# A decoder layer on one core: the first row tiles issued by two queues, and thirty transposes of the identity ahead of the first real ones

## The chip, the cores and the metric

The kernel runs on one core of a Trainium2 chip. A core has five engines with an instruction queue each: TensorE (PE in the profile; the loading of its weights is shown apart, as PEld), VectorE (DVE), ScalarE (ACT), GpSimd (POOL) and SyncE (SP), which here only issues DMAs. The metric is the device time in microseconds (us) of one execution, as the median of several.

## The reference

One decoder layer in float32 for 16 sequences of 256 tokens with 256 channels (4096 tokens), three parts, each added to its input and normalised:

```python
x = layernorm(x + attn(x))      # fixed keys and values
x = layernorm(x + xattn(x, ctx, ctx, frac))   # 16 heads, softmax, clipped position bias
x = layernorm(x + ffn(x))       # 256 -> 1024 -> 256, top-1 of 8 low-rank experts

def attn(r):                    # 4 heads of 64 channels
    q = (normalise(r) * ln_g + ln_b) split in heads
    k = w_fc.reshape(-1, 64)                  # 1024 keys, no projection of tokens
    v = w_proj.T.reshape(-1, 64)
    return r + square(relu(q @ k.T)) @ v
```

The change touches only the beginning of `attn` for the first 512 tokens.

## The kernel before

The tokens are handled in eight blocks of 512, each as four row tiles of 128 tokens x 256 channels. The program is in three stages: the first attention over the eight blocks (until about 257 us), the cross attention over 64 groups of heads, in whose gaps the feed-forward part of finished blocks is placed, and the feed-forward part of what is left. All is written out by hand in one order (`tc.manual_schedule()`, L895); each engine executes its own instructions in the order in which the Python program emits them, and waits by semaphores for what it needs. Other things than order are not planned.

The start, in the order of emission (L896 to L901):

- `rows_in[0].load()` (L257 to L263): the first block's four row tiles, each 128 KB, as four DMAs on SP's queue.
- `load_first()` (L81 to L84): the keys `kT` as two DMAs of 256 KB on SP's queue (the same keys for both halves of the partitions), and the values `vv`, 256 KB, on ACT's queue. Ahead of these, at L75 to L78, ACT has already issued the two small columns `ln_g` and `ln_b` (1 KB each) and the load of its function table.
- `rows_in[1].load()`: the second block, one DMA of 512 KB on SP's queue.
- `rows_in[0].begin()` (L275): mean and variance of each row tile on DVE (`row_stats`, L187 to L190), the inverse root by a logarithm and an exponential on ACT and three small DVE steps (`inv_std`, L192 to L210), a fourth for the shift (L244), then the rows scaled: tiles 0 and 1 on ACT (L249), tiles 2 and 3 on DVE (L287).
- `turn_in(0)` and `turn_in(1)` (L292): four transposes each on PE, of the scaled rows against the identity `ident` (L295), then gain and shift on the way out of PSUM, by ACT (L299) for the first half of the channels, by DVE (L304) for the second.

The identity is made by POOL among its first instructions (L61 to L62, `make_identity`).

Then the loop over blocks (L916), eight steps `m` for each. A step emits two `scores` (L309: four matmuls of 64 x 64 x 512 in the quarters of the array into one of two PSUM buffers, relu on ACT at L322, the square on DVE at L324), then the two `values` (L327) of the step before, then other work of that step from the list `steps`: `load_cross` (L110: weights and constants of the cross attention, all on SP's queue) in step 0 of block 0, `load_ffn` in step 2, statistics of the next block in steps 3 and 4. `values` adds up in two PSUM tiles, `tile_v()` and `tile_v("W")`.

A float32 matmul appears in the profile as two rows; a transpose as one. So one `scores` is eight rows of L314, in two groups of four that start within 20 ns of each other.

Of the kernel before, what the change touches and what calls it, by code (L numbers as in the profile page):

```python
# [9 lines left out]
FP = mybir.dt.float32  # L10
# [3 lines left out]

P = 128
EPS = 1e-5
CLAMP = 0.2
BIG = 3.0e38

# [2 lines left out]
def tile_decoder_layer(ctx: ExitStack, tc: tile.TileContext, a: dict, out: bass.AP):  # L22


    nc = tc.nc
# [4 lines left out]
    CC = C // P  # L30
# [9 lines left out]
    const = ctx.enter_context(tc.tile_pool(name="const", bufs=1))  # L40
# [16 lines left out]
    def tile_v(tag="V"):  # L57
        return psV.tile([P, 512], FP, tag=tag, name="ps_v")


    ident = const.tile([P, P], FP, name="ident")  # L61
    make_identity(nc, ident)  # L62
    epst = const.tile([P, 1], FP, name="epst")
    nc.gpsimd.memset(epst, EPS)
    rev = const.tile([P, 4, E], FP, name="rev")
    for e in range(E):
        nc.gpsimd.memset(rev[:, :, e : e + 1], float(E - e))
    def columns(name, src, eng):
        t = const.tile([P, src.shape[1]], FP, name=name)
        eng.dma_start(out=t, in_=src)  # L70
        return t


    kT = const.tile([P, 4, C], FP, name="kT")
    ln_g = columns("ln_g", a["ln_g"], nc.scalar)  # L75
    ln_b = columns("ln_b", a["ln_b"], nc.scalar)

    nc.scalar.preload_act_table_set("natural_log_exp_and_others")  # L78
    vv = const.tile([P, CC, C], FP, name="vv")

    def load_first():  # L81
        for h in range(2):
            nc.sync.dma_start(out=kT[64 * h : 64 * h + 64], in_=a["kT"])
        nc.scalar.dma_start(out=vv, in_=a["vv"].rearrange("(c p) f -> p c f", p=P))  # L84


    W = E + ER
    wq, wk, wv, wo = (const.tile([P, CC, C], FP, name=n) for n in ("wq", "wk", "wv", "wo"))
# [20 lines left out]

    def load_cross():  # L110
        load = nc.sync.dma_start
        for t, n in ((wk, "wkT"), (wv, "wvT"), (wq, "wqT")):
            load(out=t, in_=a[n].rearrange("(c p) f -> p c f", p=P))
        for t, n in ((bq, "bq"), (bk, "bk"), (fcol, "frac_cols")):
            load(out=t, in_=a[n])
        for t, n in (
            (bo, "bo"), (apos, "alpha_pos"), (aneg, "alpha_neg"), (gamma, "gamma"),
            (delta, "delta"),
        ):
            load(out=t, in_=a[n].to_broadcast(list(t.shape)))  # L120

        wo_view = a["woT"].rearrange("(o g i d) f -> i g d o f", o=CC, g=4, i=2)
        bv_view = a["bv"].rearrange("x (o g i d) -> i g d (x o)", o=CC, g=4, i=2)
        for i in range(2):
            for g in range(4):
                rows = slice(64 * i + 16 * g, 64 * i + 16 * g + 16)
                load(out=wo[rows], in_=wo_view[i, g])
                load(out=bvc[rows], in_=bv_view[i, g])
# [74 lines left out]
    def newton(mv, near, n):  # L203

        t = small.tile([P, n], FP, tag="sd", name="sd")
        nc.vector.scalar_tensor_tensor(t, mv[:, :, 1], EPS, near, ALU.add, ALU.mult)
        nc.vector.scalar_tensor_tensor(t, t, -0.5, near, ALU.mult, ALU.mult)
# [13 lines left out]
    x_view = a["x"].rearrange("(b j p) c -> b p j c", j=4, p=P)  # L221

    def tile_x():
        return px.tile([P, 4, C], FP, tag="x", bufs=3, name="x")
# [11 lines left out]
    if True:  # L236
# [16 lines left out]
        class Block:  # L253
# [3 lines left out]
            def load(self):  # L257
                self.x = tile_x()
                if self.tb:
                    nc.sync.dma_start(out=self.x, in_=x_view[self.tb])  # L260
                else:
                    for j in range(4):
                        nc.sync.dma_start(out=self.x[:, j, :], in_=x_view[0, :, j, :])  # L263

            def measure(self, jj):
                for j in range(2 * jj, 2 * jj + 2):
# [114 lines left out]
        rows_in = [Block(tb) for tb in range(NB)]  # L381
# [5 lines left out]
    if True:  # L387

        vaug = []
        for i in range(2):  # L390
            t = const.tile([P, 2, NH, 2 * HD], FP, name=f"vaug{i}")
# [4 lines left out]
        class Batch:  # L396
# [107 lines left out]
            def clip(self, name):  # L504

                t = self.cut(name, *((0.0, -CLAMP) if name == "dneg" else (CLAMP, 0.0)))
                if 2 <= self.b < MADE:
# [386 lines left out]

    with tc.manual_schedule():  # L895
        rows_in[0].load()  # L896
        load_first()
        rows_in[1].load()
        rows_in[0].begin()
        rows_in[0].turn_in(0)  # L900
        rows_in[0].turn_in(1)  # L901
# [14 lines left out]
        for tb in range(NB):  # L916
# [63 lines left out]
            for m in range(8):  # L980
                c, n2 = divmod(m, 4)
# [279 lines left out]
```

## Time and profile before

| | us |
|---|---|
| median of 3 runs (lowest, highest) | 914.74 (914.54, 915.02) |
| the profiled execution | 914.93 |
| its span, first to last instruction | 913.1 |
| TensorE busy | 892.4 |
| first matmul | 8.60 |
| first scores (L314) | 10.77 |
| first values (L334) | 16.52 |
| last matmul ends | 907.8 |

All times within a run count from the start of the span. Rows of the time line give start, busy time, engine (SPq and ACTq are the queues from which SP and ACT issue DMAs), line, operation and tiles, how many instructions are merged, and in brackets how long the engine rested before and what ended that rest. Rows of a line by form give, for instructions of one form in a window, how many, then the least, median and longest duration in ns, and first and last start. A matmul's row begins when PE takes it up; rows overlap, so the distance between starts shows the pace.

### The profile page before, as it was taken

To read this page: it belongs to the slowest core of one execution; us is meant where nothing else is said; L and a number is where in the kernel's file an instruction comes from. 1 tells how busy PE (TensorE), PEld (TensorE's weight loads), DVE (VectorE), ACT (ScalarE), POOL (GpSimd) and SP (SyncE) were. 2 spreads that over 40 slices of the span, in tenths; PEclk is the share of its full clock that TensorE was granted. 3 is DMA by queue.
4 is the path that set the end of the run, shared out by engine and by line. 5 is a ranking of instruction groups with operands and counts; after the bars stand their busy time and mean duration, and the time that the engine had idled before them with its cause. 6 is when DMAs were issued, how large, how long until landed. Compare 5 with 4: busy or idle time off the path is not lost.

```text
span 913.1 us, 19025 instructions
## 1 busy us (share of the span) xinstructions
PE 892.4 (98%) x6910; PEld 541.6 (59%) x6910; DVE 707.7 (78%) x1968; ACT 584.2 (64%) x977; POOL 379.5 (42%) x369
## 2 busy tenths in 40 slices
PE   6999999999999999999999999999999999999997
PEld 2333333333356776577658757865875686586555
DVE  5788899889878998778777877777787787678443
ACT  4757877787687879466666856665685567556111
POOL 1002312231469996434635543463454336244010
PEclk9999999999999999999999999999999999999999
DMA  5411011100001222010111202011120201111001
GB/s 137 146 36 35 30 36 41 65 1 2 3 11 50 70 71 56 13 42 21 35 43 39 52 13 66 18 37 41 40 52 14 65 17 40 41 27 45 23 1 47
DMA packets 44190, 37.01 MB, mean 41 GB/s; under 512 B 14912, under 2 KB 40000, under 8 KB 44096
## 3 DMA queue, kind: packets, MB, share of 16 engines
q1 hardware_dynamic: 43536, 35.52, 14.0%
q8 instruction: 55, 0.90, 0.4%
q14 instruction: 39, 0.32, 0.1%
q10 hardware_dynamic: 560, 0.26, 0.1%
HBM read 21.07 MB, written 6.03 MB: 30 GB/s over the span
## 4 chain that ended last, share of the span: by engine, by line
PE 56%; ACT 4%; DVE 1%; issue 1%; ACTq 0%; DVEq 0%
PE ps_b L860 12%; PE ps_l L830 12%; PE ps_b L649 9%; PE ps_l L609 6%; PE ps_v L665 5%; PE ps_b L561 3%; PE ps_b L457 2%; PE ps_b L479 2%; PE ps_l L842 2%; ACT ps_l L600 2%; ACT pT L656 1%; PE ps_b L437 1%; PE ps_b L749 1%; ACT qT L447 1%; DVE neg L624 1%
## 5 line engine op out<-in xcount | busy, mean ns | idle before, releaser
L588 POOL TENSOR_SCALAR neg<-dneg,aneg,delta 128x512 f32<-128x512 f32 x205 | 175.7, 869 | 211.2 <-ACT pT L656 185.8
L624 DVE CUSTOM_DVE_ANT_0 neg<-ps_l,neg 128x256 f32<-128x256 f32 x512 | 181.6, 420 | 43.0 <-PE ps_l L609 39.8
L600 ACT ACTIVATE ps_l<-dpos,apos_d 128x512 f32<-128x512 f32 x256 | 173.1, 686 | 34.5 <-DVE mx L624 30.5
L656 ACT ACTIVATE pT<-ps_b 128x512 f32<-128x512 f32 x256 | 143.3, 590 | 59.1 <-PE ps_b L649 57.4
L324 DVE TENSOR_TENSOR pr<-r 128x1024 f32<-128x1024 f32 x128 | 155.5, 1255 | 32.4 <-ACT r L322 32.1
L322 ACT ACTIVATE r<-ps_a 128x1024 f32<-128x1024 f32 x128 | 126.5, 1022 | 59.1 <-PE ps_a L314 33.9
L649 PE MATMUL ps_b<-ident,neg 128*128 128x128 f32 x1024 | 140.3, 278 | 4.0 <-ACT pT L656 2.4
L649 PEld LDWEIGHTS ps_b<-ident,neg 128*128 128x128 f32 x1024 | 112.9, 140 | 41.9 <-issue 15.3
L639 POOL TENSOR_TENSOR neg<-neg,mx 128x1024 f32<-128x1024 f32 x65 | 124.3, 1914 | 30.0 <-DVE mx L624 24.0
L314 PE MATMUL ps_a<-xnT,kT 64*64 64x512 f32 x1024 | 124.2, 601 | 0.0
L334 PE MATMUL ps_v<-pr,vv 64*64 64x512 f32 x1024 | 123.5, 593 | 0.3
L860 PE MATMUL ps_b<-wof,hT 128*128 128x256 f32 x512 | 115.8, 380 | 0.0
L830 PE MATMUL ps_l<-xt,wi 128*128 128x512 f32 x256 | 115.0, 596 | 0.8 <-ACT hT L849 0.8
L860 PEld LDWEIGHTS ps_b<-wof,hT 128*128 128x128 f32 x512 | 96.4, 190 | 16.0 <-issue 2.3
L639 DVE TENSOR_TENSOR neg<-neg,mx 128x1024 f32<-128x1024 f32 x63 | 90.9, 1443 | 0.3
L349 POOL TENSOR_TENSOR xt<-xt,half 128x512 f32<-128x512 f32 x15 | 23.7, 1583 | 141.0 <-ACT half L348 141.0
L334 PEld LDWEIGHTS ps_v<-pr,vv 64*64 64x64 f32 x1024 | 38.1, 132 | 70.7 <-issue 43.7
L314 PEld LDWEIGHTS ps_a<-xnT,kT 64*64 64x64 f32 x1024 | 38.1, 135 | 67.9 <-issue 56.2
L830 PEld LDWEIGHTS ps_l<-xt,wi 128*128 128x128 f32 x256 | 46.8, 190 | 52.0 <-issue 45.8
L609 PE MATMUL ps_l<-kM,qT 32*128 32x256 f32 x1024 | 74.8, 401 | 0.4 <-ACT ps_l L600 0.4
L665 PE MATMUL ps_v<-pT,vaug 128*32 128x256 f32 x1024 | 69.8, 385 | 0.8 <-ACT pT L656 0.8
L853 DVE TENSOR_SCALAR hT<-ps_l,wib 128x512 f32<-128x512 f32 x44 | 30.5, 745 | 42.8 <-PE ps_l L842 42.8
(107 smaller groups left out, 966.9 us busy)
## 6 DMA issues: line engine op xcount, KB each, us to landing
cT<-in_ctxT SPq DMA_DIRECT2D x16, 256.0 KB
kM<-keys SPq DMA_DIRECT2D x128, 32.0 KB
v<-raw SPq DMA_DIRECT2D x128, 32.0 KB
invs<-rows SPq DMA_DIRECT2D x128, 32.0 KB
x<-in_x SPq DMA_DIRECT2D x7, 512.0 KB
out<-x SPq DMA_DIRECT2D x7, 512.0 KB
frow<-in_frac SPq DMA_DIRECT2D x16, 128.0 KB
wi<-in_wiT SPq DMA_DIRECT2D x1, 1024.0 KB
```

What stands on the lines that cost most here:

```text
L314: nc.tensor.matmul(sc[64 * k : 64 * k + 64, h, :], lhsT=kT[64 * h : 64 * h + 64, q, hf * P + 64 * k : hf * P + 64 * k + 64], rhs=self.xnT[ ...
L324: nc.vector.tensor_tensor(pr, r, r, ALU.mult)
L334: nc.tensor.matmul(self.acc[k][64 * h : 64 * h + 64, :], lhsT=vv[64 * k : 64 * k + 64, hf, 64 * q : 64 * q + 64], rhs=pr[64 * k : 64 * k + ...
L588: nc.gpsimd.tensor_scalar(self.neg[:, g], self.batch.dneg, aneg[:, h : h + 1], delta, ALU.mult, ALU.mult,)
L600: nc.scalar.activation(banks[g], self.batch.dpos.rearrange("p j k -> p (j k)"), AF.Copy, scale=apos_d[:, h : h + 1],)
L609: nc.tensor.matmul(banks[g][:, j * S : (j + 1) * S], lhsT=self.batch.qT[rows, self.o, j * P : (j + 1) * P], rhs=self.batch.kM[rows, self.i ...
L624: nc.vector.tensor_tensor_reduce(out=self.t[:, g, j, :], in0=banks[g][:, j * S : (j + 1) * S], in1=self.neg[:, g, j, :], scale=1.0, scalar ...
L639: eng.tensor_tensor(rows, rows, top.to_broadcast([P, 4, S]), ALU.subtract)
L649: nc.tensor.transpose(ps[:, k * S + j * P : k * S + (j + 1) * P], self.t[:, g, j, k * P : (k + 1) * P], ident,)
L656: nc.scalar.activation(self.pT[:, g, :], self.ps[g], AF.Exp)
L830: nc.tensor.matmul(banks[g], lhsT=wi[:, c, f * P : (f + 1) * P], rhs=self.xT[:, c, :], start=(c == 0), stop=False,)
L860: nc.tensor.matmul(ps[:, 0:C], lhsT=self.hT[f][:, j * P : (j + 1) * P], rhs=wof[:, f, :], start=(f == 0), stop=(f == FC - 1),)
```

## The change

- Row tiles 1 and 3 of the first block are issued by ACT, tiles 0 and 2 by SP.
- The second block's load follows directly on SP's queue.
- `ln_g`, `ln_b` and the table load are issued behind ACT's two row tiles; the keys `kT` move from SP's queue to ACT's, behind these.
- The values `vv` move from ACT's queue to SP's, as the first of `load_cross`.
- Thirty transposes of the identity against itself are put on PE's queue ahead of the first real ones. They write in turn the four quarters of one PSUM tile, of the tag "W", that nobody reads.

```diff
+WARM = 30
-    def columns(name, src, eng):
-        t = const.tile([P, src.shape[1]], FP, name=name)
-        eng.dma_start(out=t, in_=src)
-        return t
...
-    ln_g = columns("ln_g", a["ln_g"], nc.scalar)
-    ln_b = columns("ln_b", a["ln_b"], nc.scalar)
-
-    nc.scalar.preload_act_table_set("natural_log_exp_and_others")
+    ln_g, ln_b = (const.tile([P, CC], FP, name=n) for n in ("ln_g", "ln_b"))
     vv = const.tile([P, CC, C], FP, name="vv")
 
     def load_first():
+        for t, n in ((ln_g, "ln_g"), (ln_b, "ln_b")):
+            nc.scalar.dma_start(out=t, in_=a[n])
+
+        nc.scalar.preload_act_table_set("natural_log_exp_and_others")
         for h in range(2):
-            nc.sync.dma_start(out=kT[64 * h : 64 * h + 64], in_=a["kT"])
-        nc.scalar.dma_start(out=vv, in_=a["vv"].rearrange("(c p) f -> p c f", p=P))
+            nc.scalar.dma_start(out=kT[64 * h : 64 * h + 64], in_=a["kT"])
...
     def load_cross():
         load = nc.sync.dma_start
-        for t, n in ((wk, "wkT"), (wv, "wvT"), (wq, "wqT")):
+        for t, n in ((vv, "vv"), (wk, "wkT"), (wv, "wvT"), (wq, "wqT")):
             load(out=t, in_=a[n].rearrange("(c p) f -> p c f", p=P))
...
                     for j in range(4):
-                        nc.sync.dma_start(out=self.x[:, j, :], in_=x_view[0, :, j, :])
+                        eng = nc.scalar if j % 2 else nc.sync
+                        eng.dma_start(out=self.x[:, j, :], in_=x_view[0, :, j, :])
...
     with tc.manual_schedule():
         rows_in[0].load()
+        rows_in[1].load()
         load_first()
-        rows_in[1].load()
+
+        idle = tile_v("W")
+        for j in range(WARM):
+            nc.tensor.transpose(idle[:, j % 4 * P : (j % 4 + 1) * P], ident, ident)
         rows_in[0].begin()
         rows_in[0].turn_in(0)
         rows_in[0].turn_in(1)
```

## The prediction

> **What bounds the kernel now.** I read the page first: how much room TensorE (PE) leaves, and where. Then the busy time by stretch.
>
> ```profile
> PE 892.4 (98%) x6910; PEld 541.6 (59%) x6910; DVE 707.7 (78%) x1968; ACT 584.2 (64%) x977; POOL 379.5 (42%) x369
> ```
>
> In the stretches the first number is the length, the second PE's busy time, the one before the last two the clock column.
>
> ```profile
> 0.00:8.60 8.60, 0.00 (x0) 0.03 (x1) 3.70 (x14) 2.53 (x5) 3.84 (x20) 1.00 0.70 192
> 8.60:15.10 6.50, 6.48 (x29) 2.76 (x32) 2.05 (x3) 2.72 (x4) 0.00 (x0) 1.00 0.65 185
> 15.10:100.00 84.90, 84.87 (x766) 31.82 (x758) 71.57 (x115) 58.70 (x79) 11.11 (x9) 1.00 0.21 62
> ```
>
> PE works 892.4 of 913.1 us. Of the 20.7 us it rests, 8.60 are the start and 5.3 the end (its last matmul is over at 907.8); from 15.1 to 100 it rests 0.03 us, from 100 to 300 2.3, to 600 3.0, to 907.8 1.5. So PE sets the end, the other engines follow it, and what is won or lost before about 18 us is carried to the end: in between there is hardly any rest in which a shift could drown.
>
> Then the time line of the start, and the matmuls of line 314 by form in three short windows.
>
> ```profile
> 2.97 0.43 DVE L189 BATCH_NORM_STATS2 st<-x 128x6 f32<-128x256 f32 x1 [2.97 <-DMA x<-in_x]
> ...
> 5.76 0.43 DVE L189 BATCH_NORM_STATS2 st<-x 128x6 f32<-128x256 f32 x1 [0.22 <-DMA x<-in_x]
> ...
> 8.60 2.15 PE L295 MATMUL ps_b<-ident,xn 128*128 128x128 f32 x8 [8.60 <-ACT xn L249]
> ...
> 8.81 0.33 SPq L120 DMA_DIRECT2D bo<-in_bo  x1
> ...
> 9.94 0.78 ACT L299 ACTIVATE xnT<-ps_b,ln_b,ln_g 128x512 f32<-128x512 f32 x1 [0.99 <-PE ps_b L295]
> ...
> 10.77 5.93 PE L314 MATMUL ps_a<-xnT,kT 64*64 64x512 f32 x32
> ...
> 18.23 1.90 PE L314 MATMUL ps_a<-xnT,kT 64*64 64x512 f32 x16
> ...
> 37.23 1.09 PE L295 MATMUL ps_b<-ident,xn 128*128 128x128 f32 x8
> ```
>
> ```profile
> L314 PE MATMUL ps_a<-xnT,kT x4: 1021/1026/1031, 14.2 to 14.3; 64*64 64x512 f32 x4
> ...
> L314 PE MATMUL ps_a<-xnT,kT x8: 597/814/1031, 14.2 to 15.1; 64*64 64x512 f32 x8
> ...
> L314 PE MATMUL ps_a<-xnT,kT x4: 589/589/589, 16.1 to 16.1; 64*64 64x512 f32 x4
> ```
>
> The same eight transposes take 2.15 us at 8.60 and 1.09 at 37.23. The same group of four matmuls takes about 1.03 us at 14.2 and 0.59 at 16.1, and groups follow each other every 0.85 us before 15.1 and every 0.43 after. PE runs at half speed up to 15.1 and at full speed from there. The clock column of the stretches reads 1.00 all along, so it does not show this; the durations do. Lifted once, the clock stays up to the last matmul.
>
> So the start has two costs: PE has nothing to do before 8.60, and then 6.5 us of it run at half speed. The chain behind 8.60: the fourth row tile lands (5.76), statistics until 6.40, logarithm and exponential on ACT and four small DVE steps until 7.82, the scaled rows, transposes.
>
> **The rows.** Now SP issues the four tiles one after the other (0.73 to 2.53 on its queue, 0.45 us each) and the values, issued by ACT at 1.68, share the wires with tiles three and four. After the change each queue issues two tiles, by 1.65, with nothing large in front. The first tile can't land earlier than now (2.97). DVE takes 0.56 us per tile (2.97, then 3.53), so with all tiles there in time the fourth begins at 2.97 + 3 x 0.56 = 4.65, 1.11 us before 5.76. Everything behind keeps its distances: the scaled rows would reach PE at 8.60 - 1.11 = 7.49. The other bound is no gain at all (8.60), if the second block's 512 KB, now directly behind on SP's queue, delays the third tile. I take 7.49, but see below: it decides nothing in the likeliest case.
>
> **The thirty transposes.** They stand in front of the real ones on PE's queue and wait only for the identity, which POOL finishes at 2.15 + 0.29 = 2.44; I let them start at 2.50. At half speed one follows another every 0.213 us (9.48, 9.70, 9.91 in the trace; so 2.15 us for eight with a first gap), at full speed every 0.109. All cold: 30 x 0.213 = 6.40, and PE is free at 8.90. That is later than the rows (7.49), so the work put in to fill a pause overruns it; the real transposes, their conversion on ACT and the scores queue behind it. Their output bank is used next by the value sums of the same engine, and in the built order no instruction of another engine waits for it.
>
> The question is whether they lift the clock. Row: PE began at 8.60 and was lifted at 15.1, 6.5 us later, or 4.3 us after its first true matmul at 10.77. The Trainium skill, "TensorE: Matmul & The Clock Gate", Part 1, says that about 3.4 us of sustained work, counted in windows that run freely, lift the clock; so 3.4 to 6.8 us after the start. Part 4 of the same page speaks against this change: transposes don't count as busy in the same way, and full clock doesn't engage for them. The trace fits both: by Part 1 the 6.5 us count from the transposes, with a window that ended at 11.7 only about three quarters filled (gaps at 8.8 and 10.6); by Part 4 the 4.3 us count from the matmuls. Part 4 gives for one transpose 275 ns, most of it read latency[...]; here they run gapless, each starting while the last is in flight, as the matmuls do. I take Part 1, without certainty.
>
> With windows of 3.4 us back from 15.1 (an estimate from that page and this trace) one ends at 4.9, too soon after 2.50 to be full, the next at 8.3. If they lie so again, 27 transposes are cold (2.50 to 8.27), three warm, and PE is free at 8.6. The ends, for windows that lie otherwise: lifted at 5.9, free at 5.9 + 14 x 0.109 = 7.4; or lifted only at 9.3, free at 8.9.
>
> **From the rows to the steady state.** Real transposes from 8.60, now warm: four in about 0.65 us, so ACT starts at 9.25 rather than 9.94, takes 0.78, and the scores start at 10.08 rather than 10.77: 0.69 us won. Then the fill of the pipeline, counted from the scores' start s at full speed: the second group of the first scores starts at 0.43 and ends 0.59 later, so relu (1.02, the next 0.97) runs 1.04 to 2.06 and to 3.03; the fourth scores wait for the second relu and run 3.07 to 3.93; squares on DVE (1.2 each) end at 3.33 and 4.53; the first values start at 3.93, the second wait for their square, 4.57 to 5.43; the fifth scores start at s + 5.43. In the trace that is 18.23 - 10.77 = 7.46. Won: 2.03 us, less than half of the cold stretch, because relu and squares do not speed up and become what the fill waits for. Fifth scores at 10.08 + 5.43 = 15.51, against 18.23: **2.7 us** in all. From there PE is full as before.
>
> **Keys and values.** The keys move from SP behind ACT's two row tiles, the two small columns and the table load; in the built order each of their two issues also waits for a row tile to land, about 3.0 and 3.6. Behind them on ACT's queue stands the logarithm, due at 5.40; 0.6 us per issue ends by about 4.3, so it isn't held. The table load (1.28) then lies at about 2.5 to 3.8, hidden too. The keys landed by 8.8 (SP's issue at 8.81 waited for them) and were wanted at 10.77. Now they share the wires with SP's 512 KB of rows, the values and three weights. Together these are 2.6 MB, as before, and the last of them landed at 12.4. An even share brings the keys' 0.52 MB at half of about 0.28 MB per us (5 to 10 us: 278 GB/s) from 4.3 on to 8.0, with about 0.5 for landing 8.5; both ends: 7.5, and 12.4 if everything else were served first. I take 8.5, before 10.08. The values follow the rows on SP and are wanted at about 14 rather than 16.5; second in that queue, they land before 10. The weights behind are first used tens of us later.
>
> **Sum.** 2.7 us less: span 910.4, the profiled execution 914.93 - 2.7 = 912.2. That execution lies 0.2 over the median of the runs, 914.74, which gives **912.0**. With the windows otherwise: lifted at 5.9, rows at 7.49 decide, scores at 8.97, 1.80 + 2.03 = 3.8 won, 910.9; lifted at 9.3, scores at about 10.4, 2.3 won, 912.4.
>
> **Rivals.** (1) The transposes do not lift the clock (0.35). PE is free at 8.90, real transposes cold without the gap at 8.8: four starts to 9.55, ended 9.97, ACT to 10.80, scores at 10.85 against 10.77, lift near 15.1 as now. All that the rows won is eaten by PE's own queue: 914.8. For it: Part 4, and that the trace has no lift at 11.7. (2) Keys late (0.08): ACT's queue is served behind SP's, PE has the converted rows at 10.03 and stands. While it stands the clock may fall; then the fill costs 7.46 again, and the kernel is slower once the keys land after 10.77, or after 18.23 - 5.43 = 12.8 if the clock holds. Keys at 12.4, clock fallen: 12.4 + 7.46 = 19.9, 1.6 later, 916.4. Against it: half a share suffices with 1.5 us to spare. (3) Rows no earlier (within the likeliest case): with PE free at 8.6, rows at 8.60 and 9.0, 0.4 less, 912.4.
>
> **How the numbers follow.** Lifted 0.57, 910.9 to 912.4 with 912.0 the likeliest; not lifted 0.35, 914.8, by where the windows fall some 0.6 either way; keys late 0.08, up to 916.4. A measurement here can tell about 0.2%, or 1.8 us, from no change. Every lifted case is beyond that; 0.02 off for a cost unseen gives faster 0.55. The unlifted case but for 0.01, and half of the keys, are within it: 0.38. Slower by more has the rest, 0.07. Cases of both signs hold the chance, so the range takes in both: 910.8 to 915.4; the likeliest case alone has 910.9 to 912.5.
>
> **What would show it.** Right: the identity's transposes 0.21 us apart and then 0.11, the eight real ones in about 1.1 us, groups of line 314's work 0.43 apart from the first, the fifth scores near 15.5. Wrong: spacing of 0.21 through all thirty and scores cold until about 15 (rival 1); PE idle between conversion and scores, released by the keys' transfer (rival 2). A fourth tile's statistics later than 4.7 would put the rows' step wrong. A fall of 2.7 at 15.5 that is not there at the end would put the claim wrong that PE carries a shift through.

## The result, and the profile after

The changed kernel takes 916.72 us (median of 12 runs, 915.41 to 917.40), the kernel before in the same comparison 914.58 (913.71 to 915.02): a ratio of 1.0023 [1.0015, 1.0032]. It is slower by 2.1 us, just over what a measurement can tell, where 912.0 was forecast. The profiled execution took 916.48 us with a span of 914.7, 1.55 us longer than before's 914.93.

The first row of the page, as it was read before:

```profile
PE 897.3 (98%) x6940; PEld 552.5 (60%) x6940; DVE 706.9 (77%) x1968; ACT 584.3 (64%) x977; POOL 379.5 (41%) x369
```

PE has its thirty instructions and 4.9 us of work more, and its idle time is 3.3 us less, so the span grew by the rest. The time line of the start says where. Its columns are the start, the busy time, and in the bracket what ended the idle time before it; rows of one kind that follow each other are joined. Because the change shifts the code, rows' statistics are now line 185, the transposes 292, the conversion 296 and the scores 311; line 109 is SP's load of the values and weights, line 80 ACT's load of the keys, line 256 the second block's, line 899 the thirty transposes.

```profile
1.64 0.43 SPq L256 DMA_DIRECT2D x<-in_x  x1
...
2.11 0.51 SPq L109 DMA_DIRECT2D vv<-in_vv  x1
...
2.49 5.72 PE L899 MATMUL ps_v<-ident 128*128 128x128 f32 x30 [2.49 <-POOL ident masks.py:199]
...
3.32 0.43 DVE L185 BATCH_NORM_STATS2 st<-x 128x6 f32<-128x256 f32 x1 [3.32 <-DMA x<-in_x]
...
3.49 1.17 ACTq L80 DMA_DIRECT2D kT<-in_kT  x2
...
4.94 0.40 DVE L185 BATCH_NORM_STATS2 st<-x 128x6 f32<-128x256 f32 x1
...
8.05 1.09 PE L292 MATMUL ps_b<-ident,xn 128*128 128x128 f32 x8
...
8.74 0.78 ACT L296 ACTIVATE xnT<-ps_b,ln_b,ln_g 128x512 f32<-128x512 f32 x1 [0.64 <-PE ps_b L292]
...
11.91 6.40 PE L311 MATMUL ps_a<-xnT,kT 64*64 64x512 f32 x32 [2.77 <-DMA kT<-in_kT]
...
12.96 0.21 PEld L311 LDWEIGHTS ps_a<-xnT,kT 64*64 64x64 f32 x8 [0.89 <-DMA kT<-in_kT]
...
19.71 2.03 PE L311 MATMUL ps_a<-xnT,kT 64*64 64x512 f32 x16
```

Up to the conversion on ACT nothing is lost against the forecast. The fourth tile's statistics start at 4.94 (5.76 before, 4.65 forecast), but the conversion starts at 8.74, where 9.25 was forecast. The thirty transposes take 5.72 us, where 6.4 would mean half speed all along, and the eight real ones take 1.09 us instead of 2.15: the clock is up, and ACT's half of the converted rows is there at 9.52. Then PE stands for 2.77 us, released by the keys' transfer. The keys come in two halves, one for each half of the partitions: the first lets two matmuls go at 11.91, the second the rest at 12.96. Before, they had landed by 8.8. The fifth scores, at 18.23 before and forecast at 15.51, start at 19.71.

The bytes that each queue moved, from the changed kernel's DMA view between 4.3 us (where the forecast let the keys begin) and 12.2 (where their last packet ends); the columns are packets, MB, and the share of the 16 DMA engines' time. The first row is the queue that SP issues to, the second ACT's:

```profile
q1 hardware_dynamic: 1875, 1.49, 72.1%
q10 hardware_dynamic: 446, 0.53, 30.3%
```

Together 2.02 MB in 7.9 us, 0.256 MB per us: close to the 0.28 of the forecast. ACT's queue got 0.53 of the 2.02, a quarter and not half. But this quarter is the mean of two stretches that have little in common. The first pair of rows is from 4.3 to 7.0 us, the second from 7.0 to 12.2:

```profile
q1 hardware_dynamic: 801, 0.79, 92.8%
q10 hardware_dynamic: 287, 0.00, 6.0%
...
q1 hardware_dynamic: 1074, 0.70, 61.3%
q10 hardware_dynamic: 159, 0.52, 42.9%
```

In the first, ACT's queue delivers only the two columns, 256 pieces of 8 bytes, and SP's queue moves almost three packets for each packet of ACT's. In the second the keys move, in pieces of 4 KB, and they get 0.52 of 1.22 MB: 0.43, not far from half. So the keys lost more by beginning late than by a small share.

And the stretches (length, then busy time and count of PE, PEld, DVE, ACT and POOL, the clock column, the DMA share, GB/s):

```profile
9.10:11.90 2.80, 0.04 (x1) 0.02 (x1) 0.83 (x2) 0.41 (x1) 0.00 (x0) 1.00 1.04 218
11.90:13.90 2.00, 1.98 (x13) 0.55 (x16) 0.00 (x0) 0.00 (x0) 0.00 (x0) 1.00 0.35 81
13.90:17.30 3.40, 3.40 (x22) 1.06 (x19) 1.67 (x2) 2.05 (x2) 0.00 (x0) 0.50 0.20 33
```

PE is idle from 9.1 to 11.9, and 2.0 us after it has begun again its clock falls to 0.50, for one stretch of 3.4 us. So the pause costs twice: the wait, and a piece of the clock that the thirty transposes had just bought.

### The profile page after: what moved, and what is told of

Read it like the earlier page. It is cut to its first block, busy times and chain, and to the rows that moved or that the text cites. A ratio compares the mean times of both kernels' runs of the same rounds, so it can differ in the third digit from the quotient of the medians.

```text
span 914.7 us, 19082 instructions
## 1 busy us (share of the span) xinstructions
PE 897.3 (98%) x6940; PEld 552.5 (60%) x6940; DVE 706.9 (77%) x1968; ACT 584.3 (64%) x977; POOL 379.5 (41%) x369
## 4 chain that ended last, share of the span: by engine, by line
PE 56%; ACT 3%; DVE 1%; issue 1%; ACTq 0%; DVEq 0%
PE ps_b L857 12%; PE ps_l L827 12%; PE ps_b L646 9%; PE ps_l L606 6%; PE ps_v L662 5%; PE ps_b L558 3%; PE ps_b L476 2%; PE ps_b L454 2%; PE ps_l L839 2%; ACT ps_l L597 1%; PE ps_b L434 1%; ACT pT L653 1%; PE ps_b L746 1%; ACT qT L444 1%; PE ps_b L421 0%
## 5 line engine op out<-in xcount | busy, mean ns | idle before, releaser
L311 PEld LDWEIGHTS ps_a<-xnT,kT 64*64 64x64 f32 x1024 | 41.4, 134 | 67.7 <-issue 52.4
L331 PEld LDWEIGHTS ps_v<-pr,vv 64*64 64x64 f32 x1024 | 41.0, 132 | 67.8 <-issue 39.1
```

Of the source, the lines that this page charges most:

```text
L311: nc.tensor.matmul(sc[64 * k : 64 * k + 64, h, :], lhsT=kT[64 * h : 64 * h + 64, q, hf * P + 64 * k : hf * P + 64 * k + 64], rhs=self.xnT[ ...
L331: nc.tensor.matmul(self.acc[k][64 * h : 64 * h + 64, :], lhsT=vv[64 * k : 64 * k + 64, hf, 64 * q : 64 * q + 64], rhs=pr[64 * k : 64 * k + ...
```

## The experiments

Two theories of why the keys are late. **A, the front of ACT's queue**: the two columns `ln_g` and `ln_b`, 128 pieces of 8 bytes each, stand directly in front of the keys. Their packets take from 4.29 to 6.94 here (2.10 to 3.15 before), and the keys' own from 7.01 to 12.17. **B, what SP now sends early**: freed of two row tiles and the keys, SP issues the second block at 1.64 and the values at 2.11, with the weights behind: about 1.5 MB beside or ahead of the keys. A third question is what each other part of the change is worth. "Before" in each line is the kernel before in the same comparison.

**1. The keys ahead of the columns, same queue.**

```diff
     def load_first():
+        for h in range(2):
+            nc.scalar.dma_start(out=kT[64 * h : 64 * h + 64], in_=a["kT"])
         for t, n in ((ln_g, "ln_g"), (ln_b, "ln_b")):
             nc.scalar.dma_start(out=t, in_=a[n])
...
-        for h in range(2):
-            nc.scalar.dma_start(out=kT[64 * h : 64 * h + 64], in_=a["kT"])
```

> The changed kernel with one thing moved: on ACT's queue the two key transfers are issued before the two small columns (1 KB each) instead of behind them. Theory A (the keys are late because they stand behind the small columns, whose 8-byte packets crawl between SP's large ones): the keys land by about 8.5 us, scores start by 9.5 instead of 11.9, the clock holds, and the fifth scores start near 15 instead of 19.7: about 4.5 us less than the changed kernel, 912. Theory B (the keys are late because SP's second block, values and weights share the wires, in whatever order ACT issues): the keys still land after 11, and the time stays at 916 to 917. Risk for both: the columns now come last, and the conversion that needs them waits.

Measured: 916.01, ratio 1.0013 [1.0006, 1.0020]; the profiled execution, 913.98, is among the fastest of its 21 (913.75 to 917.81), so the view shows the kind of the wait and not its usual length. The keys are now in time (packets 4.98 to 8.83). Its time line shows the conversion:

```profile
10.76 0.78 ACT L296 ACTIVATE xnT<-ps_b,ln_b,ln_g 128x512 f32<-128x512 f32 x1 [2.02 <-DMA ln_b<-in_ln_b]
```

What stood second in ACT's queue is late instead: the columns hold the conversion for 2.02 us, and the scores start at 11.59. A swap inside the queue moves the wait to another load. Neither theory is separated by it, but a queue in which whatever comes last is late speaks for B.

**2. The thirty transposes alone, added to the kernel before.**

```diff
+        idle = tile_v("W")
+        for j in range(WARM):
+            nc.tensor.transpose(idle[:, j % 4 * P : (j % 4 + 1) * P], ident, ident)
         rows_in[0].begin()
```

> The kernel before with the thirty transposes alone; all DMAs as before. Both theories of the keys expect them at about 8.8, in time. If the transposes lift the clock and the loss of the changed kernel is the keys' alone: real transposes from about 8.6, scores near 10.1, fifth scores near 15.5, 2.7 us less than before, 911.9. Rival theory C (the transposes themselves cost, because the clock they lift falls again before the work comes): clock at half speed again in the fill, 914.5 to 916.

Measured: 912.93, ratio 0.9981 [0.9972, 0.9989], so 1.8 us faster than before's 914.72. In its profile (913.92):

```profile
2.49 5.13 PE L903 MATMUL ps_v<-ident 128*128 128x128 f32 x30 [2.49 <-POOL ident masks.py:199]
```

5.13 us for thirty is again less than 6.4: the clock lifts, here about 5.9 us into the program. In this execution the rows landed late (fourth tile 6.79, before 5.76), which is why its span shows less than the median.

**3. The changed kernel without the thirty transposes.**

```diff
-        idle = tile_v("W")
-        for j in range(WARM):
-            nc.tensor.transpose(idle[:, j % 4 * P : (j % 4 + 1) * P], ident, ident)
```

> The changed kernel without the thirty transposes: its DMA order alone. Theories A and B: scores wait for the keys until about 11.9 as in the changed kernel, now cold, the fill takes 7.5 us as before, fifth scores near 19.4: 1.1 us slower than before, 915.7, and up to 1 us faster than the changed kernel or equal to it, since there most of the fill was cold too. If the transposes' lift still helped in the changed kernel, this is slower than it, 917.5.

Measured: 917.28, ratio 1.0025 [1.0017, 1.0033]; profiled 917.57.

```profile
12.48 6.90 PE L311 MATMUL ps_a<-xnT,kT 64*64 64x512 f32 x32 [2.62 <-DMA kT<-in_kT]
```

The wait for the keys is there without the transposes: 2.62 us. So the new order of the loads makes the loss. Compared with the changed kernel, the transposes bring 0.6 us where they brought 1.8 alone; 0.6 is too little to be told from nothing by the intervals of the two runs.

**4. The changed kernel with the keys back on SP's queue, ahead of the second block.**

```diff
-            nc.scalar.dma_start(out=kT[64 * h : 64 * h + 64], in_=a["kT"])
+            nc.sync.dma_start(out=kT[64 * h : 64 * h + 64], in_=a["kT"])
...
         rows_in[0].load()
-        rows_in[1].load()
         load_first()
+        rows_in[1].load()
```

> The changed kernel with the keys back on SP's queue, in front of the second block; the split of the rows, the values' place and the transposes stay. Theories A and B both expect the keys early (about 6 to 7.5), since nothing large or small stands in front of them but two row tiles: real transposes at about 8.0, scores near 9.5, fifth scores near 15: 3.3 us less than before, 911.3. If moving the keys is not the cause of the loss, the time stays near 916.7.

Measured: 912.34, ratio 0.9971 [0.9960, 0.9982]; profiled 912.21. Its time line:

```profile
1.64 1.21 SPq L80 DMA_DIRECT2D kT<-in_kT  x2
...
2.49 4.85 PE L899 MATMUL ps_v<-ident 128*128 128x128 f32 x30 [2.49 <-POOL ident masks.py:199]
...
9.69 1.95 PE L311 MATMUL ps_a<-xnT,kT 64*64 64x512 f32 x16 [0.43 <-ACT xnT L296]
...
15.47 1.90 PE L311 MATMUL ps_a<-xnT,kT 64*64 64x512 f32 x16
```

PE is released by the conversion, not by a DMA; the fifth scores start at 15.47, 2.76 us before those of the kernel before. In this profile all of the forecast gain is there once the keys come in time; by the medians it is 914.72 - 912.34 = 2.4 of the 2.7, and 1.0 less than was expected of this run.

**5. The columns on SP's queue, behind the second block.** If A is the cause, this cures it.

```diff
-            nc.scalar.dma_start(out=t, in_=a[n])
+            nc.sync.dma_start(out=t, in_=a[n])
```

> The changed kernel with the two small columns issued on SP behind the second block, so that on ACT's queue the keys follow the row tiles directly; keys, values and transposes otherwise as changed. Theory A (the small columns in front hold up the keys): the keys begin at about 4.5 to 5 and land by about 9.3, as with the keys first; the columns now crawl behind 512 KB on SP but come before 9; scores at 9.5 to 10, fifth scores near 15.2, 912 to 912.5. Theory B (SP's large transfers starve whatever ACT issues): keys land after 11, 916 or more.

Measured: 913.17, ratio 0.9985 [0.9978, 0.9991]; profiled 913.15. The keys are in time, but the columns again are not: the conversion waits 1.58 us for `ln_b` and starts at 9.72.

```profile
9.72 0.78 ACT L296 ACTIVATE xnT<-ps_b,ln_b,ln_g 128x512 f32<-128x512 f32 x1 [1.58 <-DMA ln_b<-in_ln_b]
```

It looks like a vote for A, and it isn't a clean one: the columns in SP's queue also put off the values (issued at 3.53 instead of 2.11) and the weights behind them (4.14 instead of 3.31, and so on), which is what B calls for.

**6. The gap filled: 28 more transposes between the real ones and the first scores**, to see what the fall of the clock costs.

```diff
         rows_in[0].turn_in(1)
+        for j in range(28):
+            nc.tensor.transpose(idle[:, j % 4 * P : (j % 4 + 1) * P], ident, ident)
```

> The changed kernel with 28 more transposes of the identity, about 3.05 us at full speed, placed between the real transposes and the first scores, where TensorE stood waiting for the keys. The DMAs are not touched, the keys still land near 11.9. If the clock falls because TensorE stood (theory: the fall costs most of what the transposes had won), it now holds through the fill: scores at 12.0, fifth scores near 12.0 + 5.4 = 17.4 instead of 19.7, 914.4. If the fall costs little or comes from elsewhere: 916.7, as the changed kernel.

Measured: 915.55, ratio 1.0010 [1.0003, 1.0016]; profiled 916.44.

```profile
13.90:17.30 3.40, 3.12 (x26) 0.91 (x30) 1.21 (x2) 1.94 (x2) 0.00 (x0) 1.00 0.23 38
```

```profile
13.90 1.94 PE L311 MATMUL ps_a<-xnT,kT 64*64 64x512 f32 x14 [0.64 <-DMA kT<-in_kT]
...
19.66 1.90 PE L311 MATMUL ps_a<-xnT,kT 64*64 64x512 f32 x16
```

The clock column stays at 1.00 where the changed kernel had 0.50. The keys' second half came at 13.90, the fifth scores 5.76 later at 19.66; in the changed kernel the same step took 19.71 - 12.96 = 6.75. So the fall cost the changed kernel 1.0 us in its profile. By the medians the filling gained 1.2, not the 2.3 that was expected of it: the wait itself stays.

**7. As 4, without the thirty transposes.**

```diff
-            nc.tensor.transpose(idle[:, j % 4 * P : (j % 4 + 1) * P], ident, ident)
```

> The kernel with the keys on SP in front of the second block (912.3 with transposes), now without the thirty transposes: the split rows alone, on a cold clock. Rows reach TensorE about 0.8 earlier than before, scores near 9.9, the fill cold, 7.5: fifth scores near 17.4, 0.8 less than before, 913.9. If the rows' split is worth nothing without the transposes: 914.7.

Measured: 914.10, ratio 0.9993 [0.9985, 1.0001]; profiled 913.39. Rows on two queues are worth about 0.5 us alone, which can't be told from nothing by this interval. Between 7 and 4 the transposes give 914.10 - 912.34 = 1.8, the same as in run 2.

**8. The columns at the very front of ACT's queue**, ahead of its row tiles.

```diff
     with tc.manual_schedule():
+        for t, n in ((ln_g, "ln_g"), (ln_b, "ln_b")):
+            nc.scalar.dma_start(out=t, in_=a[n])
         rows_in[0].load()
```

> The changed kernel with the two small columns at the head of ACT's queue, before its row tiles, as they stood in the kernel before. Theory A: early, with little else on the wires, they cost about 1 us; the keys begin at about 5 and land by 9.5; row tiles 1 and 3 come 0.9 later, so scores near 10.5, fifth scores near 16, 913. Theory B: keys after 11, 916 or more.

Measured: 914.79, ratio 1.0003 [0.9995, 1.0011]; the profiled execution, 913.96, is again among the fastest, here of 13 (913.94 to 915.72). The keys are in time in it, and now ACT's row tiles are late: the fourth tile's statistics start at 6.96 instead of 4.94, the scores at 11.61.

```profile
6.96 0.43 DVE L183 BATCH_NORM_STATS2 st<-x 128x6 f32<-128x256 f32 x1
```

It is the third load in turn that is late for its place.

**9. SP's stream held back**: everything on SP from the second block on is issued only after the first rows' statistics (a write of one column on DVE makes it wait); ACT's queue stays as changed, columns in front.

```diff
+                if self.tb == 1:
+                    nc.vector.memset(self.x[:, 0, 0:1], 0.0)
                 if self.tb:
                     nc.sync.dma_start(out=self.x, in_=x_view[self.tb])
...
                 for jj in range(2):
                     self.measure(jj)
+                rows_in[1].load()
...
         rows_in[0].load()
-        rows_in[1].load()
```

> The changed kernel, but SP's second block is issued only after the statistics of the first rows: a one-column memset on VectorE, put right behind them, makes its issue wait until about 5.5, and the values and weights behind it on SP's queue with it. ACT's queue is as changed, columns in front of the keys. If the columns crawl only because SP's large packets run beside them: columns done within 1 to 1.5 us as in the kernel before, keys begin near 4.5 and land by 8.5 to 9, scores near 9.5, fifth scores near 15, 912.3. If the order on ACT's queue alone delays the keys (8-byte packets slow by themselves, or the late issue behind the table load): keys still land after 10.5, 915 or more. Values and second block now land later, by about 9 to 10, still before their use at 13.5 and 26.

Measured: 912.23, ratio 0.9974 [0.9965, 0.9983]; profiled 912.51. Its time line, where the scores are now line 314:

```profile
2.67 1.82 ACTq L80 DMA_DIRECT2D kT<-in_kT  x2
...
6.13 0.39 SPq L258 DMA_DIRECT2D x<-in_x  x1
...
10.09 1.95 PE L314 MATMUL ps_a<-xnT,kT 64*64 64x512 f32 x16 [0.43 <-ACT xnT L299]
...
15.87 1.90 PE L314 MATMUL ps_a<-xnT,kT 64*64 64x512 f32 x16
```

And its DMA view between 2.6 and 6.9 us, in which the columns and all of the keys move (the columns from 3.33 to 4.82, 1.5 us against 2.65 in the changed kernel, the keys from 3.98 to 6.89, 2.9 us against 5.2):

```profile
q10 hardware_dynamic: 699, 0.75, 61.3%
q1 hardware_dynamic: 194, 0.17, 11.4%
```

With the same queue in the same order the keys come five microseconds earlier, because nearly nothing of SP's is on the wires. This is the run that decides for B: the columns still stand in front, and the time is that of run 4 (912.34) within the noise.

**10. The columns replaced by constants**, 1 and 0, set on DVE, with no DMA at all; this leaves the gain and shift of the first norm out.

```diff
-        for t, n in ((ln_g, "ln_g"), (ln_b, "ln_b")):
-            nc.scalar.dma_start(out=t, in_=a[n])
+        nc.vector.memset(ln_g, 1.0)
+        nc.vector.memset(ln_b, 0.0)
```

> The changed kernel without the two small columns' loads: gain and shift are set to 1 and 0 by VectorE, so that part of the computation is left out; keys, values, rows and transposes as changed. If the columns are what stands in front of the keys: keys begin at about 4 and land by 9 to 9.5, nothing waits for columns, scores at 9.2 to 9.7, fifth scores near 15, 912. If SP's traffic alone is enough to hold the keys: keys land after 11, 916 or more.

Measured: 915.72, ratio 1.0014 [1.0007, 1.0021]; profiled 915.48. A row of its time line, then of its list of waits over the first 20 us (total, times, longest):

```profile
12.49 1.94 PE L311 MATMUL ps_a<-xnT,kT 64*64 64x512 f32 x14 [1.48 <-DMA kT<-in_kT]
```

```profile
PE ps_a L311 <- DMA kT<-in_kT: 2.2, 2, 1.5
```

With nothing in front, the keys' packets begin at 5.16 instead of 7.01, and yet end at 11.94 instead of 12.17; PE still waits 2.2 us for them. By the medians this run is 1.0 us faster than the changed kernel (916.72 to 915.72), of 4.4 that lie between that and run 4. So A alone is not the cause. But 1.0 us is not the price of the columns either, because the edit changes SP's stream too. First a row of the changed kernel's list of SP's waits, then two of this run's DMA view between 5.2 and 11.9 us:

```profile
SPq L109 <- DMA ln_g<-in_ln_g: 2.3, 1, 2.3
```

```profile
q1 hardware_dynamic: 1473, 1.14, 70.1%
q10 hardware_dynamic: 157, 0.52, 27.6%
```

In the changed kernel SP waits 2.3 us for the first column before it issues the third weight, at 6.83. Without columns it issues it at 4.26, and 1.14 MB instead of 0.70 move beside the keys. Run 5 also takes the columns from ACT's queue, but puts the values off: there the keys move from 3.79 to 9.52, and the time is 2.6 us shorter.

**11. Only values and weights held**, until the first rows' statistics; the second block goes at once.

```diff
                 for jj in range(2):
                     self.measure(jj)
+                nc.vector.memset(vv[:, 0, 0:1], 0.0)
```

> The changed kernel with the values, and the three weights behind them on SP's queue, held until the statistics of the first rows (a one-column memset on VectorE, near 5.5); the second block's 512 KB goes out at once as changed, and ACT's queue is as changed. If the keys' lateness follows the bytes that SP has put on the wires before and beside them, this lies between the changed kernel (1.5 MB, keys about 11.9) and the one with all of SP held (keys about 7.4): keys at 8.5 to 9.5, scores at 9.5 to 10, 912.3 to 913. If the second block alone is what holds them up, they still land after 11 and the time is 915.5 to 916.7.

Measured: 912.53, ratio 0.9976 [0.9966, 0.9986]; profiled 913.39, the slowest of its nine.

```profile
10.91 0.21 PEld L312 LDWEIGHTS ps_a<-xnT,kT 64*64 64x64 f32 x8 [1.02 <-DMA kT<-in_kT]
```

The keys' second half came at 10.91 in that profile, so PE still lost about 1 us there; the median can't be told from run 9's. It is the megabyte of values and weights, which is wanted last, more than the second block's half megabyte, that had taken the keys' place. No run held the second block alone.

**12. The changed kernel once more, unchanged**, for the scatter of its own.

> The changed kernel once more, for a second trace. The keys should again be what the first scores wait for, landing at 11 to 14; the clock lifts within 3 to 6 us of the first transpose and falls for one window of 3.4 us only if TensorE stood through most of one. 916 to 917.

Measured: 916.46, ratio 1.0018 [1.0012, 1.0025]; profiled 915.83. From its time line:

```profile
11.71 1.04 PE L311 MATMUL ps_a<-xnT,kT 64*64 64x512 f32 x2 [2.15 <-DMA kT<-in_kT]
...
13.38 1.94 PE L311 MATMUL ps_a<-xnT,kT 64*64 64x512 f32 x14 [0.63 <-DMA kT<-in_kT]
```

The keys' second half is later still (13.38), but PE's pause is cut in two pieces, 2.15 and 0.63 us, and the clock doesn't fall: the fifth scores follow at 19.13, 5.75 after the second half. So the wait for the keys is there in both traces of this kernel, and the fall of the clock in one. The mean clocks of this run's 18 executions suggest how often it falls: eight have 0.999 or 1.000 and take 914.5 to 915.8 us, ten have 0.995 to 0.998 and take 916.4 to 917.7. (One stretch of 3.4 us at half speed takes 0.5 x 3.4 / 914 = 0.002 off the mean clock.)

## Why the prediction was wrong, step by step

**PE sets the end and carries a shift through: right.** The profiled time less the start of the fifth scores is 896.70 us before, 896.77 after, and in eleven of the twelve experiments between 896.57 and 896.84 (run 10, with its constants, 897.23). So all that follows is decided by about 20 us, and the fifth scores can stand for the time.

**The rows: right in direction, too much in size.** The forecast kept the first tile's landing as it was before (2.97); it came at 3.32. From there DVE took 0.54 per tile, and the fourth began at 4.94 where 4.65 was reckoned, later than the 4.7 that the forecast had named as the sign that this step is wrong. Worth by run 7: 0.5 us, which can't be told from nothing.

**The transposes lift the clock: right; the size was off.** In all eleven profiles that have them, the clock lifts 2.8 to 5.7 us after the first of them (5.3 to 8.2 us into the program, forecast 8.3 with 5.9 to 9.3 as ends). What Part 4 of "TensorE: Matmul & The Clock Gate" of the Trainium skill says of transposes doesn't hold for this gapless stream. The gain is 1.8 us in two pairs of runs (2 against before, 4 against 7), and with the 0.5 of the rows 2.3, where 2.7 was reckoned for both together. The warm fill was put at 5.43 and measured 5.78 in runs 4 and 9: 0.35 too little.

**"An even share brings the keys' 0.52 MB at half of about 0.28 MB per us from 4.3 on to 8.0, with about 0.5 for landing 8.5": this is the step that failed**, and mostly in its start. The forecast let the keys move as soon as they were issued, at 4.3, and gave the two columns in front of them on ACT's queue no time at all. The keys' first packet moved at 7.01, right behind the columns' last (6.94) and 2.71 later than forecast. Then 0.52 MB took 5.16 us instead of 3.7, 1.46 longer: 0.43 of 0.235 MB per us instead of half of 0.28. Last, PE was released 0.79 after the last packet instead of 0.5, 0.29 later. Together this is 4.46 us, from 8.5 to 12.96.

The even share itself had a point in the trace of before, from 3.2 to 5.0 us, where the values on ACT's queue ran beside SP's row tiles:

```profile
q10 hardware_dynamic: 272, 0.26, 42.4%
q1 hardware_dynamic: 230, 0.22, 38.3%
```

What that trace did not have were small pieces on ACT's queue beside a long stream on SP's: its columns moved among the first loads, from 2.10 to 3.15. The stream is behind both larger terms: with it held back (run 9) the keys' first packet moves at 3.98, and all of them take 2.91 us.

A landing at 12.4 was the forecast's own second rival, at 0.08, with its price: 916.4, against 916.72 measured. Its reason, "ACT's queue is served behind SP's", points to the right stream, but does not hold as it stands, since the keys got 0.43 of the bytes while they moved. And its time is near by luck: the keys came later than 12.4, and only one stretch of the fill was cold (6.75 us, not 7.46). The Trainium skill, "DMA: Bandwidth & Descriptors", section "Issuing engines are not separate DMA queues", says that the DMAs of all engines run on the same 16 DMA engines and interleave there, and that issuing from several saves issue time only. Runs 9 and 10 agree: on a queue of their own the keys' 0.52 MB took 6.8 us beside SP's stream (run 10), and 2.9 us with that stream held (run 9).

The error can be closed as a sum. The fifth scores were forecast at 15.51 and came at 19.71, 4.20 later. 2.88 of it is the keys' second half at 12.96 instead of scores at 10.08; 1.0 the fall of the clock in the pause (runs 6 and 12 have the same step without it); 0.3 the fill. In run 4, where the keys are in time, the whole of the rest stands: profiled 912.21 where 912.2 was forecast. That agreement is partly luck, since PE was free earlier than reckoned (scores 9.69, not 10.08) and the fill longer by 0.35.

Not settled: the fall costs 1.0 us in the one profile that shows it, while the medians of run 12's two groups lie 1.9 apart. That profile (916.48) would be among the fastest of the slower group, and no trace shows one from its middle, so whether the clock falls there for longer or the keys come still later is open. Also open: in what order the DMA engines take the pieces of two queues. That the wires are served in the order of issue across queues would fit the changed kernel and runs 9 and 11. It doesn't explain why the keys in run 8, issued at 3.08, came in time, and in run 10, issued from 1.70, did not.

Runs 4 and 9 beat both kernels: 912.34 and 912.23, ratios 0.9971 [0.9960, 0.9982] and 0.9974 [0.9965, 0.9983]; run 11's 912.53 can't be told from them. Both keep the thirty transposes and the rows on two queues, and see to it that what is wanted last is issued last.

## What to carry to other kernels

When a load moves off a queue, look first at what that queue now sends early: the loss here was not where the keys went but what took their place on the wires. Write down for each early load when it is wanted, and issue in that order over all queues together; a queue of its own keeps no load clear of another queue's stream. Give a small load that stands in front of a large one a time of its own in the sum: here 2 KB in front of the keys took 2.65 us beside the other queue's stream. Work that warms PE's clock pays if the real work follows without a pause: here 1.8 us when it did, and when it didn't 0.6, which can't be told from nothing.

## What the runs showed of the hardware

- The clock changes at the edges of windows of 3.41 us. In each of the fourteen profiles the time from the first lift to the last fall is a whole number of them: 897.71 us in the kernel before is 263 x 3.4133, 904.53 in run 4 is 265 x 3.4133. This agrees with the Trainium skill, "TensorE: Matmul & The Clock Gate", Part 1, which has freely running windows of about 3.4 us.
- A window need not be full to lift the clock. In run 4 the first edge came 2.83 us after the first transpose, and the clock rose there; in run 9 it came 2.27 us after it, and the clock rose only at the next. So the lift, 2.8 to 5.7 us after the first transpose, is a matter of where the edge happens to lie. In the kernel before, 3.1 us of PE's rows in the window up to 11.70, with gaps between the first transposes, did not lift it, so the busy time of the rows is no exact measure.
- The clock fell after a pause of 2.8 us, though no window was empty. The lifts and the fall of the changed kernel (7.10, 13.92, 17.34) put an edge at 10.51, inside the pause, with some 1.4 us of it on each side. The clock came back by itself after one window, at a cost of 1.0 us. In run 12's profile a pause of 2.15 and one of 0.63 did not bring it down. What decides is open: by its rows PE worked 2.0 us of the window that ended at 13.92, and only 1.5 us of one in run 12 (8.05 to 11.47) that brought no fall.
- The clock column of the stretches reads 1.00 from 2.5 to 7.1 us in the changed kernel, while the first transposes run at 0.213 us each. In these traces it says nothing before the first lift or fall on record; the spacing of equal instructions does.
- Two loads of 1 KB in 8-byte pieces took 1.05 us early in the kernel before (2.10 to 3.15), and 2.65 us in the changed one beside the bulk loads (4.29 to 6.94). They can hold up a queue, or be held up (runs 1 and 5), far beyond their size.
